# Issuing a two-layer attention and expert kernel's second attention in the written order

## The chip, the cores and the metric

The kernel runs on one core of one Trainium2 chip. The metric is the device time of one execution in microseconds, the median of the runs. Engines are named as the profile names them: PE (matmuls and transposes), DVE (VectorE), ACT (ScalarE), POOL (GpSimd), SP (SyncE, which here only issues DMAs). Each has its own queue of instructions and works through it in order; an instruction that has to wait for another engine or a DMA holds back whatever stands behind it in the same queue.

## The reference

Four blocks in a row are added to x, which has 4 batches of 512 rows of 256 numbers, in f32. ctx is a context of 4 batches of 1601 rows.

```python
x = x + L0_xattn(ctx, layernorm(x))   # 8 heads of 128, keys from context and x
x = x + L0_ffn(layernorm(x))          # top-2 of 8 experts, with a capacity for each
x = x + L1_xattn(ctx, layernorm(x))   # 8 heads of 32, keys from the context
x = x + L1_ffn(layernorm(x))          # top-2 of 8 experts by a threshold, no capacity
```

The change lies in the third, the second attention: q = layernorm(x) Wq, k = ctx Wk, v = ctx Wv, eight heads of 32, softmax over 1601 keys, no output projection.

## The kernel before, in words

Stage a is the first attention, stage b the first experts, stage c the second attention, stage d the second experts. PE ends stage b at 1927 us of the span. The change concerns stage c, and the work of its neighbours that runs inside it.

**Units and rounds.** The second attention is cut into 16 units: 4 batches, two groups of four heads (o), two halves of the queries (f, 256 each). A unit has NM = 13 key tiles of 128. A loop advances by two key tiles at a time; here one pass is called a round, and there are 104 of them with weights in them. Its counter, step, counts key tiles over all units.

**What a round holds.** `weights(u, j)` multiplies keys by queries into a PSUM tile ps_w (L1119) and ACT takes Exp of it into pT (L1132). The row maximum enters through an extra row of the queries (`asked`), so that ACT's Exp needs no further operand. `weigh` (L1150) multiplies pT, one round later, with v into ps_o. `add_weights` (L1141) adds pT to a running sum for the softmax's denominator, on DVE for the even tiles and on POOL for the odd tiles 3 to 11. pT has six buffers. `maxima(u, g)`, eight for each unit and done during the unit before, computes the scores of a quarter of the keys into two PSUM tiles ps_s (L1072), which DVE reduces to maxima (L1080). When a unit's eight are there, `negated` (L1089) reduces them to `shift`, and `to_row` (L1102, L1106) transposes them on PE and copies the row into `asked` on ACT. ps_s, ps_w and the PSUM tiles of the side work all come from one pool of three two-bank buffers (ps_s, tag s); the smaller ones of the closing come from a single buffer (ps_m).

**Closing.** When a unit's keys are done, `closing` copies ps_o (L1162), sums the denominators on PE (ps_n, L1168), copies them (by, L1177), transposes both (tp_o, L1182 and L1183), and on DVE takes reciprocals (L1192), scales (got, L1194) and adds to x (L1201).

**Side work, dealt out by step.** `put` and `spread` place generators' pieces in a table `at` by step: `collect` clears 8 tiles (L284) and gathers the first experts' results of the next batch into them with indirect DMAs on POOL (L285), `add_collected` adds them to x on DVE (L301), `queries` normalizes x (L93 to L116), transposes it (L130) and projects it (ps_q, L1021). `keys_values` of batches 2 and 3 (L873, L889) also runs here. `route2` is the second experts' routing of a batch whose attention is done: layernorm into `pay`, with a number of the lane beside it (L354, L362), transposes, scores (ps_l, L372), the choice of two experts in some thirty small DVE operations (L394 to L429), counts on PE (ps_c, L432), the places (L441 to L444), eight indirect DMAs on POOL that scatter `pay` to rows_x in DRAM (L446), and a bias through PE (L459 to L470).

**What sets the order.** SP's, PE's, DVE's, ACT's and POOL's instructions are traced in the order that the loop writes them, and a scheduler then orders each engine's queue by its own expectation of times. So the written order is a suggestion: what has no dependency may be moved up far ahead of its place. Sizes of instructions and buffers are as written.

Of the kernel before, what the change touches and what calls it, by code (L numbers as in the profile page):

```python
# [16 lines left out]
P = 128  # L17
# [44 lines left out]


@with_exitstack
def xattn_ffn_twice(ctx: ExitStack, tc: tile.TileContext, a: dict, out: bass.AP):
    nc = tc.nc

# [3 lines left out]
    ident = const.tile([P, P], F32, name="ident")  # L71
    make_identity(nc, ident)

# [26 lines left out]

    def ln_scale(pool, mv, n):
        ve = pool.tile([P, n], F32, tag=f"ve{n}", name="ve")
        nc.vector.tensor_scalar(ve, mv[:, :, 1], EPS, None, ALU.add)
        rs = pool.tile([P, n], F32, tag=f"rs{n}", name="rs")
        nc.scalar.activation(rs, ve, AF.Sqrt)
        nc.vector.reciprocal(rs, rs)

        t = pool.tile([P, n], F32, tag=f"nt{n}", name="t")
        nc.vector.tensor_tensor(t, rs, rs, ALU.mult)
        nc.vector.tensor_tensor(t, t, ve, ALU.mult)  # L110
        nc.vector.tensor_scalar(t, t, -0.5, 1.5, ALU.mult, ALU.add)
        nc.vector.tensor_tensor(rs, rs, t, ALU.mult)
        return mv, rs
# [163 lines left out]
    def collect(b):  # L277

        got = []
        for t in range(NT):  # L280
            for k in range(2):
                j = b * NT + t
                g = gat.tile([P, D], F32, tag="g", name="g")
                nc.vector.memset(g, 0.0)  # L284
                nc.gpsimd.indirect_dma_start(  # L285
                    out=g,
                    out_offset=None,
                    in_=slot_y[:, :],
                    in_offset=bass.IndirectOffsetOnAxis(ap=slot[k][:, j : j + 1], axis=0),
                    bounds_check=SLOTS - 1,  # L290
                    oob_is_err=False,
                )
                got.append(g)
        return got

    def add_collected(b, got):
        for t in range(NT):
# [49 lines left out]
    def route2(b, two, psum, tag, first=0, n=NT):  # L347
# [40 lines left out]

        yield

# [14 lines left out]

        yield

# [14 lines left out]

        yield

# [12 lines left out]
        )  # L437
        yield
        for k in range(2):
# [15 lines left out]
        yield  # L455

# [5 lines left out]
        for t0 in range(0, n, 2):  # L462
# [474 lines left out]
    with ExitStack() as st:  # L937
# [44 lines left out]

        got0 = collect(0)

# [6 lines left out]
    with ExitStack() as st:  # L991
# [19 lines left out]
        def queries(b, qT):  # L1011
            xn = one.tile([P, NT, D], F32, tag="xn", name="xn")
            layernorm(two, xn, x[b], NT)
            yield
# [143 lines left out]
        def closing(u, ps):  # L1158
# [3 lines left out]
            nc.scalar.copy(oT, ps)  # L1162
            yield
            ps = ps_m.tile([P, QH], F32, tag="m", name="ps_n")
            for k in range(2):
                for i in range(HG):
# [7 lines left out]
                    )  # L1174
            yield
            by = one.tile([P, QH], F32, tag="by", name="by")
# [4 lines left out]
            for t in range(2):  # L1181
# [7 lines left out]
                )  # L1189
            yield  # L1190
            inv = two.tile([P, 2 * HG], F32, tag="inv", name="inv")
# [102 lines left out]
        if to_close:  # L1294
            for _ in to_close:
                pass
        assert not at, sorted(at)

# [3 lines left out]
    with ExitStack() as st:  # L1302
# [151 lines left out]
        nc.vector.tensor_copy(n_over_i, n_over)  # L1454
        ties = nc.values_load(n_over_i[0:1, 0:1], min_val=0, max_val=E * T)
        spare = st.enter_context(tc.tile_pool(name="d_spare", bufs=1))
# [135 lines left out]
```

## Time and profile before

| | us |
|---|---|
| four runs | 3068.07, 3066.93, 3063.63, 3064.47 |
| median | 3065.7 |
| the profiled execution | 3066.01 |
| its span | 3064.3 |
| second attention, first weights to the last sums | 1996.0 to 2677.4 |

A profile is of one execution. Its page gives busy time of each engine, the chain of work and the costliest groups; the trace can be asked for windows, for the waits of an engine and for single instructions in order of time. A timeline row reads: start and duration in us, engine, line, operation, out<-in, sizes, count of instructions put together, and in brackets the idle time of that engine before it and what ended it. Line numbers are those of the kernel before.

### The profile page before, as it was taken

The numbers are of one execution on the slowest core, as the hardware profiler recorded it, in microseconds if no ns is written. First come the engines' busy times: TensorE is split into PE (matmuls) and PEld (weight loads), VectorE is DVE, ScalarE is ACT, GpSimd is POOL, SyncE is SP. The second block draws the span as 40 slices with busy tenths as digits, with TensorE's granted clock in tenths as the row PEclk, the third lists the DMA queues.
The fourth block names the chain that finished last, engine by engine and source line by source line (L and its number), as shares of the span: only waits on it lengthen the run. The fifth ranks groups of instructions, "written<-read, shape, count | busy, mean of one in ns | idle before, by whom it ended". The sixth has DMA issues, their size and how long they took to land. (4 is left out here: it accounts for less than half of the span.)

```text
span 3064.3 us, 35871 instructions
## 1 busy us (share of the span) xinstructions
PE 2833.9 (92%) x13564; PEld 1888.0 (62%) x13564; DVE 1436.5 (47%) x2351; ACT 932.7 (30%) x1328; POOL 476.0 (16%) x347
## 2 busy tenths in 40 slices
PE   5899999999999999999997999599989897859999
PEld 2566666666666667666664666344544444448888
DVE  4365456544565454454443000677657566621111
ACT  2233234233342333323221211144344343412221
POOL 1000000100001000010001000333333333434442
PEclk9999999999999999999997999699999898869999
DMA  8543343344433433333333331300010100045562
GB/s 301 182 115 99 99 109 89 103 101 101 110 89 102 103 95 92 87 106 99 92 99 117 120 110 57 84 16 18 17 44 15 34 15 23 12 159 186 171 194 72
DMA packets 160941, 293.94 MB, mean 96 GB/s; under 512 B 42824, under 2 KB 78014, under 8 KB 157560
## 3 DMA queue, kind: packets, MB, share of 16 engines
q1 hardware_dynamic: 118280, 181.12, 21.4%
q0 software_dynamic: 17904, 74.77, 7.7%
q10 hardware_dynamic: 24576, 35.68, 4.4%
q8 instruction: 108, 1.77, 0.2%
q14 instruction: 73, 0.60, 0.1%
HBM read 100.24 MB, written 42.69 MB: 47 GB/s over the span
## 5 line engine op out<-in xcount | busy, mean ns | idle before, releaser
L687 DVE TENSOR_REDUCE top<-ps_s 128x1 f32<-128x2113 f32 x128 | 301.8, 2358 | 580.9 <-PE ps_s L679 577.5
L716 PE MATMUL ps_o<-pT,v 128*128 128x256 f32 x2176 | 521.2, 382 | 7.9 <-DVE pT L708 7.9
L679 PE MATMUL ps_s<-kT,qT 128*128 128x512 f32 (+1 forms) x1280 | 489.6, 527 | 14.8 <-ACT attn L693 14.5
L716 PEld LDWEIGHTS ps_o<-pT,v 128*128 128x128 f32 x2176 | 411.1, 191 | 125.0 <-issue 69.9
L679 PEld LDWEIGHTS ps_s<-kT,qT 128*128 128x128 f32 x1280 | 242.0, 191 | 264.5 <-issue 240.1
L693 ACT ACTIVATE attn<-ps_s,top 128x2113 f32<-128x2113 f32 x128 | 259.0, 2024 | 475.4 <-DVE top L687 412.5
L708 DVE STREAM_TRANSPOSE pT<-swapped 128x2176 f32<-128x2176 f32 x128 | 312.4, 2441 | 58.2 <-DMA swapped<-attn 47.9
L1080 DVE TENSOR_REDUCE tops<-ps_s 128x2 f32<-128x800 f32 (+1 forms) x256 | 243.2, 983 | 87.3 <-PE ps_s L1072 86.9
L1119 PE MATMUL ps_w<-asked,keyed 64*128 64x256 f32 (+1 forms) x1664 | 244.8, 426 | 39.8 <-DVE tops L1080 38.3
L629 PE MATMUL ps_k<-kvin,wkv 128*128 128x512 f32 (+1 forms) x640 | 261.5, 533 | 4.3 <-ACT kT L636 4.3
L1141 POOL TENSOR_TENSOR sum<-sum,pT 128x1024 f32<-128x1024 f32 x80 | 200.2, 2503 | 395.0 <-PE ps_o L1150 206.0
L662 PE MATMUL ps_v<-wkv,kvin 128*128 128x256 f32 x1088 | 253.5, 381 | 0.0
L1132 ACT ACTIVATE pT<-ps_w 128x1024 f32<-128x1024 f32 (+1 forms) x176 | 176.6, 1023 | 223.9 <-PE ps_w L1119 222.0
L1119 PEld LDWEIGHTS ps_w<-asked,keyed 64*128 64x128 f32 (+1 forms) x1664 | 157.4, 197 | 133.8 <-DVE tops L1080 74.1
L662 PEld LDWEIGHTS ps_v<-wkv,kvin 128*128 128x128 f32 x1088 | 204.9, 190 | 32.7 <-issue 3.3
L1072 PE MATMUL ps_s<-kT,qT 32*128 32x400 f32 (+1 forms) x1024 | 162.1, 588 | 26.7 <-DVE tops L1080 24.5
L1141 DVE TENSOR_TENSOR sum<-sum,pT 128x1024 f32<-128x1024 f32 x96 | 141.1, 1469 | 92.7 <-ACT pT L1132 79.5
L636 ACT ACTIVATE kT<-ps_k,bqk 128x512 f32<-128x512 f32 (+1 forms) x160 | 97.2, 621 | 267.0 <-PE ps_k L629 121.2
L629 PEld LDWEIGHTS ps_k<-kvin,wkv 128*128 128x128 f32 x640 | 116.2, 191 | 80.1 <-issue 67.0
L1417 PE MATMUL ps_h<-xT,w_e 128*128 128x256 f32 x736 | 163.7, 381 | 0.0
L1436 PE MATMUL ps_y<-w_e,hT 128*128 128x256 f32 x736 | 162.5, 379 | 0.0
L1417 PEld LDWEIGHTS ps_h<-xT,w_e 128*128 128x128 f32 x736 | 140.7, 191 | 19.3
(239 smaller groups left out, 2611.1 us busy)
## 6 DMA issues: line engine op xcount, KB each, us to landing
swapped<-attn SPq DMA_DIRECT2D x1536, 68.0 KB
swapped<-attn ACTq DMA_DIRECT2D x512, 68.0 KB
rows_x<-empty SPq DMA_DIRECT2D x32, 530.0 KB
w<-in_w_dram SPq DMA_DIRECT2D x16, 1024.0 KB
cT<-in_ctxT_dram SPq DMA_DIRECT2D x4, 1601.0 KB
keyed<-kT SPq DMA_DIRECT2D x32, 200.1 KB
ctx_b<-in_ctx_dram SPq DMA_DIRECT2D x4, 1536.0 KB
slot_x<-empty POOLq DMA_DIRECT2D x8, 512.0 KB
```

Of the source, the lines that this page charges most:

```text
L629: nc.tensor.matmul(ps[:, :n], lhsT=wkv[:, c, hs], rhs=flat_kvin[c][:, j0 : j0 + n], start=c == 0, stop=c == DC - 1,)
L662: nc.tensor.matmul(ps[:, k, :], lhsT=flat_kvin[c][:, j * P : (j + 1) * P], rhs=wkv[:, c, cols], start=c == 0, stop=c == DC - 1,)
L679: nc.tensor.matmul(flat[:, j0 : j0 + n], lhsT=qT[:, t * P : (t + 1) * P], rhs=kT[:, j0 : j0 + n], start=True, stop=True,)
L687: nc.vector.tensor_reduce(top, flat[:, :L], AX.X, ALU.max, negate=True)
L693: nc.scalar.activation(attn[:, :L], flat[:, :L], AF.Exp, bias=top, accum_out=total)
L708: nc.vector.transpose(pT[:, :, k * P : (k + 1) * P].rearrange("p c (a i) -> p a c i", a=4), swapped.rearrange("p a (c i) -> p a c i", i=32),)
L716: nc.tensor.matmul(ps, lhsT=v[:, j - parts[part][0], (h % 2) * DH0 : (h % 2 + 1) * DH0], rhs=pT[:, j, :], start=j == 0, stop=j == NB - 1,)
L1080: nc.vector.tensor_reduce(tops[u][:, t, 2 * pair : 2 * pair + 2, k], pss[pair][:, :, : hi - lo], AX.X, ALU.max,)
L1119: nc.tensor.matmul(ps[:r, s, pair * QH : (pair + 1) * QH], lhsT=keyed[o][64 * s : 64 * s + 64, pair, j * P : j * P + r], rhs=asked[u % 3][ ...
L1132: nc.scalar.activation(pT[:r], ps[:r], AF.Exp)
L1141: (nc.gpsimd if k else nc.vector).tensor_tensor(to, to, pT[:r], ALU.add)
L1417: nc.tensor.matmul(ps[:, f, :], lhsT=w[:, at : at + P], rhs=xT[:, c, :], start=c == 0, stop=c == DC - 1,)
```

## The change

An object with the four engines takes the place of `nc` and, while a flag is set, tells the scheduler of every instruction traced on PE, DVE, ACT and POOL that it has to stay behind the one traced before it on its engine. The flag is set from the first unit's maxima to the end of the second attention's loop. SP's DMAs are not held. The write order in the loop is changed with it: of a round's maxima the first stands ahead of the weights and the others behind them, and the adds of pT stand one round earlier and ahead of `weigh`. Closing is done in three pieces, at its step, 4 and 6 steps later. `to_row` stands one step earlier. `collect` is dealt out one gather to a step, `add_collected` one tile to two steps, and `queries` and `route2` are cut at other places, mostly where work passes from one engine to another, and dealt out one piece to two steps: `queries` in 5 pieces from step 22 of a batch (4 from 18), `route2` in up to 16 from step 10 (8, one to a step, from 12), with one scatter to a piece. All from the softmax's weights (L400) over the choice of experts and the counts on PE to the places, which were in four pieces before, is now one piece.

```diff
+class InOrder:
...
+    def __getattr__(self, name):
+        f = getattr(self.engine, name)
+        def call(*args, **kwargs):
+            ins = f(*args, **kwargs)
+            if self.kept[0]:
+                self.tc.keep_in_program_order(ins)
+            return ins
+        return call
...
 def xattn_ffn_twice(ctx: ExitStack, tc: tile.TileContext, a: dict, out: bass.AP):
-    nc = tc.nc
+    nc = Engines(tc)
...
-    def ln_scale(pool, mv, n):
+    def ln_root(pool, mv, n):
         ve = pool.tile([P, n], F32, tag=f"ve{n}", name="ve")
         nc.vector.tensor_scalar(ve, mv[:, :, 1], EPS, None, ALU.add)
         rs = pool.tile([P, n], F32, tag=f"rs{n}", name="rs")
         nc.scalar.activation(rs, ve, AF.Sqrt)
+        return ve, rs
+
+    def ln_scale(pool, mv, n, root=None):
+        ve, rs = root or ln_root(pool, mv, n)
         nc.vector.reciprocal(rs, rs)
...
     def collect(b):
...
+        return got, [lambda t=t, k=k: one_of(t, k) for t in range(NT) for k in range(2)]
...
-        mv, rs = ln_stats(two, xb, n)
+        mv = ln_moments(two, xb, n)
+        root = ln_root(two, mv, n)
+        yield
+        mv, rs = ln_scale(two, mv, n, root)
...
-        yield
 
         lg, wb, keep, rest = wide("lg"), wide("wb"), wide("keep"), wide("rest")
...
         nc.scalar.activation(wb, wb, AF.Exp)
+        yield
         nc.vector.tensor_tensor(wb, wb, keep, ALU.mult)
...
         nc.vector.tensor_copy(pay[:, :, D + 1 :], wb)
 
-        yield
 
         nc.vector.tensor_copy(rest, keep)
...
         nc.vector.tensor_tensor(extra[:, mine_b, :], rest, wb, ALU.mult)
 
-        yield
...
             ps.rearrange(flat), lhsT=ones, rhs=earlier.rearrange(flat), start=False, stop=True
         )
-        yield
         for k in range(2):
             off, place, at = small("off2"), wide("place"), place2[k][:, mine_b]
...
             nc.vector.tensor_copy(at, off)
+        yield
+        for k in range(2):
+            at = place2[k][:, mine_b]
             for t in range(n):
                 nc.gpsimd.indirect_dma_start(
...
-
-        yield
+                yield
+
...
             nc.vector.tensor_tensor(xs, xs, ps, ALU.add)
+            yield
...
         for u in range(1, n_units):
-            for g in range(2 * HG):
-                put(NM * u - 5 - NM + (g * NM) // (2 * HG), lambda u=u, g=g: maxima(u, g))
             put(NM * u - 5, lambda u=u: negated(u))
-            put(NM * u - 3, lambda u=u: to_row(u))
+            put(NM * u - 4, lambda u=u: to_row(u))
...
-                spread(s0 + 12, route2(b - 1, one, ps_s, "s"))
+                spread(s0 + 10, route2(b - 1, one, ps_s, "s"), 2, 16)
             if b + 1 < B:
-                got = []
-                put(s0 + 1, lambda b=b, got=got: got.extend(collect(b + 1)), lambda b=b: begin(b + 1))
-                put(s0 + 16, lambda b=b, got=got: add_collected(b + 1, got))
+                put(s0 + 1, lambda b=b: begin(b + 1))
+                got, steps = collect(b + 1)
+                for k, f in enumerate(steps):
+                    put(s0 + 1 + k, f)
+                for t in range(NT):
+                    put(
+                        s0 + 14 + 2 * t,
+                        lambda b=b, got=got, t=t: add_collected(b + 1, got, (t,)),
+                    )
...
-                spread(s0 + 18, later(), 2, 4)
+                spread(s0 + 22, later(), 2, 5)
...
-        spread(per_batch * (B - 1) + 2 * NM + 12, last_half, 1, 8)
+        spread(per_batch * (B - 1) + 2 * NM + 11, last_half, 1, 14)
...
+        nc.kept[0] = True
         for g in range(2 * HG):
             maxima(0, g)
         negated(0)
         to_row(0)
-        for step in sorted(k for k in at if k < 0):
-            for f in at.pop(step):
-                f()
+
+        ahead = {}
+        for u in range(1, n_units):
+            for g in range(2 * HG):
+                step = NM * u - 5 - NM + (g * NM) // (2 * HG)
+                ahead.setdefault(max(step, 0) // 2, []).append((u, g))
 
         held = []
-        to_add = []
-        to_close = None
-        for step in range(0, NM * n_units + 6, 2):
+        for step in range(0, NM * n_units + 10, 2):
+            first, *more = ahead.pop(step // 2, [None])
+            if first:
+                maxima(*first)
             fresh = []
             for k in range(step, step + 2):
                 u, j = divmod(k, NM)
                 if u < n_units:
                     fresh.append((u, j, weights(u, j)))
-            if to_close:
-                if next(to_close, 1):
-                    to_close = None
+            for g in more:
+                maxima(*g)
+            for h in held:
+                add_weights(*h)
             for uw, jw, pT in held:
...
                 if jw == NM - 1:
-                    to_close = closing(uw, ps_of)
-                    next(to_close)
-            for h in to_add:
-                add_weights(*h)
+                    ending = closing(uw, ps_of)
+                    next(ending)
+                    put(step + 4, lambda ending=ending: next(ending))
+                    put(step + 6, lambda ending=ending: next(ending, None))
...
-            held = to_add = fresh
+            held = fresh
...
+        nc.kept[0] = False
```

The new names: `ahead` holds the maxima by round, and `ending` a closing's generator. Those maxima that fall ahead of the first step go to round 0. Apart from order, the instructions are the same ones.

More of the change, by code (lines that the diff above doesn't have):

```diff
@@ L61, in rows_of, with __init__ @@
     return tail if i == n - 1 else P
+class InOrder:
+    def __init__(self, tc, engine, kept):
+        self.tc, self.engine, self.kept = tc, engine, kept
+    def __getattr__(self, name):
[6 more added lines that the diff above has]
+        return call
+class Engines:
+    def __init__(self, tc):
+        self.kept = [False]
+        self.tensor, self.vector, self.scalar, self.gpsimd = (
+            InOrder(tc, e, self.kept) for e in (tc.nc.tensor, tc.nc.vector, tc.nc.scalar, tc.nc.gpsimd)
+        )
+        self.sync = tc.nc.sync
 @with_exitstack
 def xattn_ffn_twice(ctx: ExitStack, tc: tile.TileContext, a: dict, out: bass.AP):
-    nc = tc.nc
+    nc = Engines(tc)
     const = ctx.enter_context(tc.tile_pool(name="const", bufs=1))
@@ L71, in xattn_ffn_twice @@
     ident = const.tile([P, P], F32, name="ident")
-    make_identity(nc, ident)
+    make_identity(tc.nc, ident)
     flip = [0]
@@ L279, in collect, with one_of, add_collected @@
         got = []
[L280 to L297, printed above, removed]
+        def one_of(t, k):
+            j = b * NT + t
+            g = gat.tile([P, D], F32, tag="g", name="g")
+            nc.vector.memset(g, 0.0)
+            nc.gpsimd.indirect_dma_start(
+                out=g,
+                out_offset=None,
+                in_=slot_y[:, :],
+                in_offset=bass.IndirectOffsetOnAxis(ap=slot[k][:, j : j + 1], axis=0),
+                bounds_check=SLOTS - 1,
+                oob_is_err=False,
+            )
+            got.append(g)
+        return got, [lambda t=t, k=k: one_of(t, k) for t in range(NT) for k in range(2)]
+    def add_collected(b, got, tiles=range(NT)):
+        for t in tiles:
             for k in range(2):
@@ L981, in xattn_ffn_twice @@
         results(*last)
-        got0 = collect(0)
+        got0, steps = collect(0)
+        for f in steps:
+            f()
     QH = 2 * P
@@ L1012, in queries @@
             xn = one.tile([P, NT, D], F32, tag="xn", name="xn")
-            layernorm(two, xn, x[b], NT)
+            mv = ln_moments(two, x[b], NT)
+            root = ln_root(two, mv, NT)
+            yield
+            mv, rs = ln_scale(two, mv, NT, root)
+            for i in range(NT):
+                ln_apply(xn, x[b], mv, rs, i)
             yield
@@ L1174, in closing @@
                     )
-            yield
             by = one.tile([P, QH], F32, tag="by", name="by")
@@ L1189, in closing @@
                 )
-            yield
             inv = two.tile([P, 2 * HG], F32, tag="inv", name="inv")
@@ L1229, in xattn_ffn_twice @@
                 put(s0, lambda b=b: load_keys(b, 1))
-                spread(s0 + 12, route2(b - 1, one, ps_s, "s"))
+                spread(s0 + 10, route2(b - 1, one, ps_s, "s"), 2, 16)
             if b + 1 < B:
-                got = []
-                put(s0 + 1, lambda b=b, got=got: got.extend(collect(b + 1)), lambda b=b: begin(b + 1))
-                put(s0 + 16, lambda b=b, got=got: add_collected(b + 1, got))
+                put(s0 + 1, lambda b=b: begin(b + 1))
[6 more added lines that the diff above has]
+                        lambda b=b, got=got, t=t: add_collected(b + 1, got, (t,)),
+                    )
                 def later(b=b):
                     yield from queries(b + 1, qTs[b + 1])
-                spread(s0 + 18, later(), 2, 4)
+                spread(s0 + 22, later(), 2, 5)
             if 1 <= b and b + 1 < B:
@@ L1292, in xattn_ffn_twice @@
                     f()
-            held = to_add = fresh
[L1294 to L1297, printed above, removed]
+            held = fresh
+        assert not at and not ahead, (sorted(at), sorted(ahead))
+        nc.kept[0] = False
     kvst.close()
@@ L1454, in xattn_ffn_twice @@
         nc.vector.tensor_copy(n_over_i, n_over)
-        ties = nc.values_load(n_over_i[0:1, 0:1], min_val=0, max_val=E * T)
+        ties = tc.nc.values_load(n_over_i[0:1, 0:1], min_val=0, max_val=E * T)
         spare = st.enter_context(tc.tile_pool(name="d_spare", bufs=1))
```

## The prediction

> **What bounds the kernel now.** I read the busy line first, then the windows around the second attention, then single rounds in the timeline, then PE's and DVE's waits.
>
> ```profile
> span 3064.3 us, 35871 instructions
> PE 2833.9 (92%) x13564; PEld 1888.0 (62%) x13564; DVE 1436.5 (47%) x2351; ACT 932.7 (30%) x1328; POOL 476.0 (16%) x347
> ```
>
> PE sets the span. The profiled execution took 3066.01 us, 1.7 more than its span and 0.3 more than the median 3065.7, so a change of the span carries over to the median as it is. About 0.2%, 6.1 us, is what a measurement of this kernel can tell from no change. The next view has, after each window, PE, PEld, DVE, ACT, POOL busy, the granted clock, DMA share and GB/s.
>
> ```profile
> 1927.00:1963.00 36.00, 7.70 (x22) 3.71 (x24) 18.96 (x65) 8.77 (x8) 17.83 (x18) 0.57 0.44 117
> 1963.00:1996.00 33.00, 29.09 (x102) 11.16 (x98) 30.66 (x72) 3.11 (x5) 14.95 (x15) 0.57 0.22 61
> 1996.00:2670.00 674.00, 603.72 (x5006) 330.38 (x5004) 449.21 (x688) 272.92 (x330) 224.58 (x106) 0.93 0.08 22
> ```
>
> The experts end at 1927, the first weights' matmul is at 1996, the last units' end is near 2677. In the long window PE idles 674.0 − 603.7 = 70.3 us; to that I add the 6.4 us stop at 2677 shown below, 77 in all. At clock 0.93 its 603.7 us hold about 561 of full-speed work, so slow clock costs 43. Only these two sums, and the 69 us of start, can be won or enlarged; the matmuls stay the same ones.
>
> An undisturbed round (two key tiles):
>
> ```profile
> 2009.86 0.95 PE L1072 MATMUL ps_s<-kT,qT 32*128 32x400 f32 x8
> 2010.75 2.29 PE L1119 MATMUL ps_w<-asked,keyed 64*128 64x256 f32 x16
> 2012.96 1.07 PE L1150 MATMUL ps_o<-pT,v 128*32 128x256 f32 x16
> 2013.96 0.96 PE L1072 MATMUL ps_s<-kT,qT 32*128 32x401 f32 x8
> ...
> 2010.85 1.89 DVE L1080 TENSOR_REDUCE tops<-ps_s 128x2 f32<-128x800 f32 x2 [0.74 <-PE ps_s L1072]
> 2012.98 1.22 DVE L1141 TENSOR_TENSOR sum<-sum,pT 128x1024 f32<-128x1024 f32 x1 [0.24 <-ACT pT L1132]
> ```
>
> By starts, PE spends 0.89 + 2.21 + 1.00 = 4.10 us. DVE needs 1.89 + 1.22 = 3.11, so about 0.9 us more DVE work in a round is free; what exceeds it makes PE wait, because scores and weights share three PSUM buffers.
>
> **The stalls there are.** DVE's waits name the largest, "pay<-lane" behind a scatter, 20.2 us in 3 times; two of them with PE's answer:
>
> ```profile
> 2417.15 0.33 DVE L362 TENSOR_SCALAR pay<-lane 128x1 f32<-128x1 f32 x4 [8.59 <-DMA rows_x<-pay,place]
> 2418.44 1.72 PE L1072 MATMUL ps_s<-kT,qT 32*128 32x400 f32 x8 [7.70 <-DVE tops L1080]
> ...
> 2604.48 0.21 DVE L362 TENSOR_SCALAR pay<-lane 128x1 f32<-128x1 f32 x2 [8.40 <-DMA rows_x<-pay,place]
> 2605.65 0.69 PE L1119 MATMUL ps_w<-asked,keyed 64*65 64x256 f32 x2 [10.19 <-DVE tops L1080]
> ```
>
> The scheduler hoisted a few-element write of the next routing far ahead; it waits until the previous scatters have read the buffer, and the reduces queue behind it. PE loses 2.30 (at 2234) + 7.70 + 10.19 = 20.2. After the 7.70 the same scores last 1.72 for 0.95: the clock halved, some 3 us more each time. The end:
>
> ```profile
> 2677.36 1.08 PE L1168 MATMUL ps_n<-sum,ones 128*32 128x256 f32 x8 [6.40 <-POOL sum L1141]
> ```
>
> Three POOL adds (7.5 us) run late behind scatters.
>
> **Part 1, the start.** Pinning ends the hoisting of later batches' gathers, memsets and layernorms into 1948–1994. The first LN's own steps from sqrt (1948.6) to transposes (1955.4) take 6.8 us of which 2.1 are its own DVE work up to the first scaled tile, and the transposes follow a like step later: −5.4. The 16 first reduces ran 1964.97 to 1986.88, 21.9 us; back to back 16 × 0.95 = 15.2: −6.7. Before, 13 maxima preceded the first weights; written order has 9, which takes the rest. First weights at about 1977 instead of 1996, −18.7. But four maxima now follow, 4 × 0.89 = +3.6, and round 0 holds five of them, whose reduces (5 × 1.89) outlast PE's work by 4.3. Net **−10.8**.
>
> **Part 2, lane waits and the end.** The write now stands in its routing, long after the previous scatters: 20.2 of idle go, and two clock tails. POOL's last adds: written order leaves the scatters of the last half-routing two rounds to finish; 1 of 6.4 stays. Both are in the sum of part 3.
>
> **Part 3, new waits.** A DVE instruction that waits for something now holds its place, and what stands behind it, mostly the two reduces, waits too. By the same DVE balance (from single durations: reduce 0.95, add 1.22, PE 4.10):
> - Rounds with two maxima, one before and one after the weights: 15 of them have no key/value projection to cover them; the second maxima's scores start 0.89 + 2.21 = 3.10 into the round, their reduces 0.99 later as above, 4.09 to 5.98, and the add ends at 7.20; the next round's scores start at 4.10 + 0.89 = 4.99 and could be reduced from 5.98. DVE is 1.22 late, and PE, out of buffers, waits as long: 15 × 1.25 = 19. The trace has such stops of 0.42 (PE's scores at 2094.76) and 1.19 (weights at 2090.66).
> - 16 closings: reciprocal 0.20, got 0.42, x add 0.42 to 2.00 between the reduces; less the free 0.9: 0.35 to 2.0, taken 0.8: 13.
> - The shift's maximum and its row now stand one step apart, often in one round: PE's transposes wait for DVE's last reduces. 7 rounds × 1.5 + 6 × 0.5 = 13.5.
> - The routing's choose chain, in one piece with PE's ps_c in its middle: 27 small DVE operations stand before ps_c, at about 0.17 each (the small rows of the layernorm lasted 0.10 to 0.20) 4.6 us. Before, its last part took 2194.18 to 2199.2, one of its operations lasting 2.35. In written order PE arrives and waits: 3 × 4.6 + the half routing with 5.3, a lock's part in it, = 19.
> - The other pieces (layernorms of three batches 5 + 2 × 3.4, routing scores 2 × 1.4 + 2.6, wbT 3 × 0.8, halves 5): 25.
> - POOL's end: 1.
> Sum 91 of idle against the 77 before: **+14**, the 20 us of lane waits being in the 77. Before has no such rows in this order, so each is bounded by 0 (side work on PE's queue covers it) and by about double (a lock in it, as the 2.35 above); no gain is possible from a wait added.
>
> **Part 4, the clock.** Four choose stalls × 3.1 = +12, lane tails −6, and PE waits less deep in its ordinary rounds: −6 taken from the 43. Net 0. The gathers, dealt one per step, I cost at nothing: their readers stand 13 steps behind the first and 12 behind the last, 25 us, and DMA share is 0.08. On POOL two gathers of 1.01 and an add of 2.35 make 4.36 in a round of 4.10, so its adds slip by 1 us over four rounds, which six pT buffers cover; without that cover it is 1 us of PE in each of three batches. SP's loads are not pinned and stand five rounds ahead of their use. Scatters stay 2.8 to 2.9 us each on POOL; their price is the last rival's.
>
> Sum: −10.8 + 14 + 0 = **+3.3: 3066 + 3 = 3069 us**, own range 3050 to 3088.
>
> [...]
>
> **Rivals.** *Faster, 3030:* adds are issued one round earlier, and collide less with POOL. Undisturbed adds take 1.22, those of the stage have mean 1.44 (79 of them), 17 us of DVE time. Units without side work took 34.8 to 37.0 us from one ps_n to the next, where 6.5 rounds × 4.10 = 26.7, 1.5 more maxima at 0.89, and 2 to 3 us of the closing's own matmuls make 31. If 8 such units fall by 3 (−24) and half-clock windows (27 × 3.41 us) lose a third, −15: −39 from 3069. For it: PE's waits on the reduces, 38.3 + 23.6. Against it: POOL's adds stay as many and as long.
>
> *Slower, 3105:* the lock.
>
> ```profile
> 2087.07 2.35 POOL L1141 TENSOR_TENSOR sum<-sum,pT 128x1024 f32<-128x1024 f32 x1 [1.75 <-ACT pT L1132]
> ...
> 2087.71 2.00 DVE L1201 TENSOR_TENSOR x<-x,got 128x256 f32<-128x256 f32 x1
> ```
>
> The x add (0.42 alone, mean 1.15 over 16) ends when the POOL add ends. In the written order both adds of a round start as the two exps end, so that a closing's x add, 2 rounds later, meets POOL each time: 16 × 1.2, and the adds of 15 double rounds × 0.55, 27 us; with clock tails of five half-rate windows, 5 × 3.1 = 16, and less 7 of the 13 that I counted for closings, +36 on 3069. It decides if the x adds' mean passes 1.15. [...]
>
> *Not what it says, 3093:* in the built order, POOL's scatters are not held behind adds: four stand in a row, 4 × 2.9 = 11.6 us before the next add; the six pT buffers, three rounds of work or 12.3 us, are then nearly used up, and ACT and after it PE would wait some 3 us in each of four routings, a clock tail of 3.1 behind it: 4 × 6 = +24.
>
> **Chances.** Own forecast 0.50 (of it 0.14 faster by over 0.2%, 0.14 within, 0.22 slower), faster rival 0.27 (0.01 of it within), lock 0.18, scatters 0.05. Faster 0.40, same 0.15, slower 0.45. The range reaches from below the faster rival to just above the lock: 3022 to 3108.
>
> **What would show it.** First weights near 1977; "pay<-lane" gone from DVE's waits; ps_c waited for about 4.6 three times; PE's transposes of the shift waiting behind double rounds; idle of the stage near 91; its last ps_n near 2680. Wrong if idle stays under 60 (faster), if x adds average over 1.15 us or clock falls below 0.91 (lock), or if PE waits for pT while POOL scatters.

## The result, and the profile after

The changed kernel takes 3071.4 us (median of 45 runs, 3061.07 to 3077.18) where the kernel before takes 3067.5 (68 runs); the ratio is 1.0011, with a 95% interval of 1.0005 to 1.0016. By the ratio that is 3.4 us more (the medians differ by 3.9), inside the 0.2% that the prediction called no change. The profiled execution took 3071.08.

The page's head and busy line:

```profile
span 3069.4 us, 35856 instructions
PE 2822.9 (92%) x13564; PEld 1878.8 (61%) x13564; DVE 1455.3 (47%) x2351; ACT 941.3 (31%) x1332; POOL 466.1 (15%) x347
```

The span is 5.1 us longer, and PE is busy 11 us less: time has gone into waiting. The windows, split at the first weights and at the last sums (columns as before):

```profile
1927.00:1969.92 42.92, 24.14 (x93) 11.18 (x93) 25.53 (x50) 10.25 (x10) 8.24 (x8) 0.60 0.28 72
...
1969.92:2682.50 712.58, 608.99 (x5044) 326.02 (x5044) 493.92 (x776) 283.01 (x338) 246.21 (x132) 0.91 0.09 24
```

The first weights come at 1969.9 instead of 1996.0, 26.1 us earlier. From there to the last sums PE idles 712.58 − 608.99 = 103.6 us, where it was 77. So the changed kernel is 26 us ahead at the first weights, loses 27 in waits behind them, and carries four more maxima there. The start, PE's and DVE's rows:

```profile
1944.13 2.14 PE L74 MATMUL tp<-ident,xn 128*128 128x128 f32 x8 [21.07 <-DVE xn L74]
...
1969.92 3.35 PE L74 MATMUL ps_w<-asked,keyed 64*128 64x256 f32 x16
...
1982.26 3.79 PE L74 MATMUL ps_w<-asked,keyed 64*128 64x256 f32 x16
...
1952.20 14.89 DVE L74 TENSOR_REDUCE tops<-ps_s 128x2 f32<-128x800 f32 x16 [5.84 <-PE ps_s L74]
```

Nothing of later batches stands between; the 16 reduces run back to back in 14.9 us. Not all of the 26 us is the change's, though. The idle time ahead of the transposes begins where PE ends the experts, at 1944.13 − 21.07 = 1923.06 here, and in the kernel before at 1927.29:

```profile
1955.42 2.14 PE L130 MATMUL tp<-ident,xn 128*128 128x128 f32 x8 [28.13 <-DVE st L93]
```

Seven of the variants below have the changed kernel's code up to there, and in their profiles the experts end at 1924.7 to 1927.5, so I take these 4.2 us for the spread between executions. Counted from the experts' end, the first weights come after 46.9 us instead of 68.7, 21.8 less, and the last sums after 759.4 us instead of 750.1, 9.3 more (the kernel before, then the changed one):

```profile
1927.29:2677.40 750.11, 640.90 (x5132) 345.44 (x5134) 501.34 (x827) 285.18 (x343) 264.51 (x140) 0.89 0.10 28
...
1923.06:2682.50 759.44, 633.13 (x5132) 337.20 (x5136) 520.09 (x827) 293.59 (x347) 254.45 (x140) 0.90 0.10 28
```

The first round lasts from 1969.92 to 1982.26, 12.3 us. It has five maxima's scores in it and no `weigh` yet: 2.21 + 5 x 0.89 = 6.7 us of work. The profile has PE idle for 0.24 us of it only, but in its middle DVE sets the pace:

```profile
1974.40:1979.40 5.00, 5.00 (x24) 1.79 (x24) 5.00 (x6) 0.00 (x0) 0.00 (x0) 1.00 0.00 0
...
1974.19 7.28 DVE L74 TENSOR_REDUCE tops<-ps_s 128x2 f32<-128x800 f32 x8 [2.28 <-PE ps_s L74]
...
1976.13 0.30 PEld L74 LDWEIGHTS ps_s<-kT,qT 32*128 32x128 f32 x4 [0.60 <-DVE tops L74]
```

The scores of four maxima go on from 1974.40 to 1982.26, 7.9 us for 3.6, and up to 1979.4 at a full clock: the weight load (PEld) of each group of four waits for a reduce, and DVE works without a gap. These 4.3 us are a wait for DVE that is counted as busy time of PE. The weights ahead of them ran at a clock of 0.58, 3.28 us for 2.21. And PE's waits (total, times, longest):

```profile
PE ps_w L74 <- DVE tops L74: 41.6, 30, 4.9
PE ps_c L74 <- DVE earlier L74: 17.8, 6, 5.6
PE ps_r L74 <- DVE shift L74: 16.3, 9, 3.0
PE tp L74 <- DVE pay L74: 6.5, 2, 4.1
PE ps_o L74 <- ACT oT L74: 6.2, 8, 0.8
PE ps_c L74 <- DVE cnt L74: 4.4, 1, 4.4
```

The 7.7 to 10.2 us stops behind the lane's write are gone, and so is the wait of DVE for the scatters. In their place stand many stops of up to 5.6 us, of the kinds shown all but one behind DVE.

### The profile page after: what moved, and what is told of

It is laid out like the page before. It is cut to its first block, busy times and chain, and to the rows that moved or that the text cites. A ratio compares the mean times of both kernels' runs of the same rounds, so it can differ in the third digit from the quotient of the medians.

```text
span 3069.4 us, 35856 instructions
## 1 busy us (share of the span) xinstructions
PE 2822.9 (92%) x13564; PEld 1878.8 (61%) x13564; DVE 1455.3 (47%) x2351; ACT 941.3 (31%) x1332; POOL 466.1 (15%) x347
## 5 line engine op out<-in xcount | busy, mean ns | idle before, releaser
L74 PE MATMUL ps_s<-kT,qT 128*128 128x512 f32 (+3 forms) x2304 | 633.9, 554 | 18.2 <-ACT attn L74 14.7
L74 PE MATMUL ps_o<-pT,v 128*128 128x256 f32 (+2 forms) x3584 | 626.8, 395 | 7.7 <-DVE pT L74 7.7
L74 PEld LDWEIGHTS ps_o<-pT,v 128*128 128x128 f32 (+2 forms) x3584 | 450.2, 161 | 179.1 <-issue 111.0
L74 PEld LDWEIGHTS ps_s<-kT,qT 128*128 128x128 f32 (+1 forms) x2304 | 292.8, 193 | 320.8 <-issue 264.9
L74 PE MATMUL ps_w<-asked,keyed 64*128 64x256 f32 (+1 forms) x1664 | 252.5, 432 | 49.5 <-DVE tops L74 41.6
L74 ACT COPY v<-ps_v 128x512 f32<-128x512 f32 (+1 forms) x165 | 91.6, 560 | 278.0 <-PE ps_v L74 210.5
L74 DVE TENSOR_TENSOR sum<-sum,pT 128x1024 f32<-128x1024 f32 x96 | 154.2, 1606 | 6.3 <-ACT pT L74 6.3
```

The costliest lines, as they stand in the source:

```text
L74: ins = f(*args, **kwargs)
```

## The experiments

Two theories were tried. One: instructions in fixed places move PE's waits, and their sum follows what DVE has to do in a round with PE's work of 4.1 to 5.0 us against it. The other: single badly placed instructions (PE's ps_c, the shift's row) cost what PE waits at them. Differences between kernels of different sets of runs are taken from their ratios to the kernel before, in parts of 3066 us.

### The adds' place in a round

```diff
-            for g in more:
-                maxima(*g)
             for h in held:
                 add_weights(*h)
+            for g in more:
+                maxima(*g)
```

> The changed kernel with DVE's and POOL's adds of pT written ahead of a round's second maxima and not behind them, so that in a round with two maxima DVE does reduce, reduce, add and then the second pair. The prediction's sum for such a round has DVE late by 1.22 us because its add comes after reduces that can't start before 4.09: by it the add falls into DVE's idle time from 2.9 to 4.1 and 15 x 1.25 = 19 us go: 3052. Rival (the add isn't ready then, because its Exp ends later, or the wait is the shift's): within 6 of the changed kernel.

3037.7 us, ratio 0.9918 (0.9901 to 0.9935): about 28 us less than the changed kernel by the ratios, and clearly faster than the kernel before. One such round in the changed kernel's timeline, DVE's rows first:

```profile
2086.68 1.89 DVE L74 TENSOR_REDUCE tops<-ps_s 128x2 f32<-128x800 f32 x2 [1.21 <-PE ps_s L74]
2087.03 2.35 POOL L74 TENSOR_TENSOR sum<-sum,pT 128x1024 f32<-128x1024 f32 x1 [3.65 <-ACT pT L74]
2088.48 1.98 DVE L74 TENSOR_TENSOR sum<-sum,pT 128x1024 f32<-128x1024 f32 x1
2090.38 0.23 DVE L74 TENSOR_REDUCE shift<-tops 128x4 f32<-128x16 f32 x2
2090.59 0.66 PE L74 MATMUL ps_r<-ident,shift 128*128 128x128 f32 x4 [2.95 <-DVE shift L74]
```

and the same round with the adds first:

```profile
2081.68 1.21 DVE L74 TENSOR_TENSOR sum<-sum,pT 128x1024 f32<-128x1024 f32 x1
...
2082.97 1.89 DVE L74 TENSOR_REDUCE tops<-ps_s 128x2 f32<-128x800 f32 x2
2083.32 2.35 POOL L74 TENSOR_TENSOR sum<-sum,pT 128x1024 f32<-128x1024 f32 x1 [3.65 <-ACT pT L74]
2084.77 0.23 DVE L74 TENSOR_REDUCE shift<-tops 128x4 f32<-128x16 f32 x2
2084.99 0.66 PE L74 MATMUL ps_r<-ident,shift 128*128 128x128 f32 x4 [1.05 <-DVE shift L74]
```

In the first, DVE idles 1.21 and then does its add when POOL's add runs, 1.98 for 1.21; in the second the add fills the idle time and meets no POOL add. PE's wait falls by 1.90, from 2.95 to 1.05. Over the stage (its window from the first weights to the last sums):

```profile
1971.40:2641.30 669.90, 589.16 (x5048) 317.90 (x5044) 490.00 (x776) 283.16 (x339) 252.71 (x132) 0.94 0.09 26
```

PE idles 80.7 us where it was 103.6, 22.9 less for the 19 that the prediction's term had. PE's busy time falls by 19.8 with the same matmuls, as the clock rises from 0.91 to 0.94. In these two executions the clock's part is nearly as large as the wait's own, and the expectation had none. But the profiled execution, 3030.5, is the fastest of its runs, 3030.5 to 3041.1, and the stage is 42.7 us shorter in it where the ratios give 28. The mean clock of a whole run is 0.962 to 0.964 in all six of them, and 0.955 to 0.962 in the changed kernel's, with a median of 0.959; 0.004 of 3050 us is 12 us, an estimate of the clock's part of the 28.

### The shift's row one step later, on top of it

```diff
-            put(NM * u - 4, lambda u=u: to_row(u))
+            put(NM * u - 3, lambda u=u: to_row(u))
```

> The changed kernel with the adds ahead of the second maxima, and the shift's row put back to one step later, as in the kernel before. In the changed kernel half of the units have the shift's maximum and the row's transposes in one round, so PE meets the transposes while DVE still reduces; 11.6 us in 9 places are left of that wait. Theory (it is only the place): they go, 3038 - 11 = 3027. Rival (PE then runs on to the next wait for DVE, which is as far behind): 3034 to 3038.

3038.4 us, ratio 0.9910 (0.9896 to 0.9924): no change against 0.9918. PE's waits at the row have fallen from 11.6 us to 1.2, and these have grown or come:

```profile
PE ps_w L74 <- DVE tops L74: 29.0, 23, 2.9
...
PE ps_s L74 <- DVE tops L74: 2.7, 2, 2.0
```

ps_w was 25.6, and ps_s behind DVE's reduces was not in the list. By the first weights of the last key tile PE has idled 77.2 us, 78.5 without the edit. The rival holds: PE runs on to the next place at which it needs DVE.

### The second unit's maxima dealt two to a round

```diff
-                ahead.setdefault(max(step, 0) // 2, []).append((u, g))
+                ahead.setdefault((g if u == 1 else step) // 2, []).append((u, g))
```

> The changed kernel with the adds ahead of the second maxima, and the second unit's eight maxima dealt two to each of the first four rounds, where the changed kernel has five in round 0 and one in the next three. In the changed kernel round 0 lasts 12.3 us where PE's work is 4.10 + 4 x 0.89 = 7.7. The prediction's step says that five pairs of reduces outlast PE's work and that this costs 4.3; with two maxima to a round DVE's 3.78 + 1.22 fits PE's 4.99: 3038 - 5 = 3033. Rival (the time there is the halved clock of a PE that waits anyway): 3038.

3033.8 us, ratio 0.9891 (0.9874 to 0.9907); its interval and the 0.9901 to 0.9935 without the edit overlap, so the median's 4 us are not shown. From the first weights to those of the second unit the trace takes 44.1 us, 43.7 without the edit. Taken by rounds, the theory holds where it was aimed: the first round takes 6.3 us instead of 11.6. That is 5.3 less for three maxima fewer, as much as their reduces take (3 x 1.8) and twice what PE's work on them would (3 x 0.89). (The expectation's 7.7 us of work has 1.0 for a `weigh` in it that this round lacks.) The halved clock of the rival was not the reason, as the row for the scores of four maxima without the edit shows, with PE and DVE both busy throughout at a clock of 1.00:

```profile
1975.91:1983.03 7.12, 7.12 (x32) 2.39 (x32) 7.12 (x9) 0.00 (x0) 0.00 (x0) 1.00 0.00 0
```

But the gain is lost at once: the next three rounds, with a maximum more in each, take 21.5 us instead of 12.7. Two maxima to a round don't fit there either, because of rows like these:

```profile
1987.96 1.01 POOL L74 DMA_INDIRECT g<-slot_y,slot  x1 [0.30 <-issue]
1988.31 4.16 DVE L74 TENSOR_TENSOR sum<-sum,pT 128x1024 f32<-128x1024 f32 x1
...
1989.00 2.38 POOL L74 TENSOR_TENSOR sum<-sum,pT 128x1024 f32<-128x1024 f32 x1
...
1993.42 0.94 PE L74 MATMUL ps_s<-kT,qT 32*128 32x400 f32 x4 [1.98 <-DVE tops L74]
```

DVE's add of 1.2 us lasts 4.16 (and again at 1996.47), over POOL's gather and then the whole of POOL's add, and PE stops behind the reduces that follow.

### The closing's add to x on POOL

```diff
-            nc.vector.tensor_tensor(
+            nc.gpsimd.tensor_tensor(
                 xs, xs, got.rearrange("p (t h) d -> p t (h d)", t=2), ALU.add
             )
```

> The changed kernel with the adds ahead of the second maxima, and the closing's add of its result to x put on POOL. On DVE that add lasts 0.42 alone and has a mean of 1.07 over 16 closings, 17 us in all, since it collides with POOL's adds of pT. Theory (in rounds with a closing DVE's total work against PE's 4.1 to 5.0 is what PE waits for, and the collisions are part of it): PE's wait falls by the prediction's 0.8 in each of 16 closings, 13 us, 3038 - 13 = 3025. Rival (on POOL the add takes its turn among POOL's adds and shuts DVE's adds out for as long, or POOL's adds come late for the closing's sums): 3034 to 3045.

3024.8 us, ratio 0.9872 (0.9854 to 0.9890): 13 to 14 us less than with the adds first alone, the fastest version here, 41 us under the kernel before. The add's rows by tile (min, median, max in ns), first with it on POOL:

```profile
L74 POOL TENSOR_TENSOR x<-x,got x16: 722/730/1646, 2042.1 to 2635.9; 128x256 f32<-128x256 f32 x16
```

and with it on DVE, adds first:

```profile
L74 DVE TENSOR_TENSOR x<-x,got x16: 424/936/3154, 2041.9 to 2643.7; 128x256 f32<-128x256 f32 x16
```

PE's waits behind the reduces, 25.6 us in 24 times, become 13.1 in 11: the 13 of the expectation. But the shift's waits grow from 11.6 to 15.1 and ps_c's by 2, so the traces' spans differ by 7.6 only; the rest of the medians' difference lies in the spread of the runs to compare with, whose profiled one is the fastest.

### The routing's chain of small operations

One cut ahead of PE's ps_c, and then three cuts:

```diff
+        yield          # chain_cut and chain_pieces
         ps = psum.tile([P, n, E], F32, tag=tag, name="ps_c2")
...
         nc.vector.tensor_copy(pay[:, :, D + 1 :], wb)
+        yield          # chain_pieces
...
         nc.vector.tensor_tensor(extra[:, mine_b, :], rest, wb, ALU.mult)
+        yield          # chain_pieces
```

> The changed kernel with one more cut in the routing, just ahead of PE's ps_c, so that PE meets ps_c one round after DVE begins the chain of small operations. Theory A (what costs is that PE's queue holds an instruction whose input is 5 us away): the waits for ps_c, 20.3 us in four places, go and some 10 us of halved clock behind them, 3071 - 30 = 3041. Rival B (what costs is the 4.6 us of DVE work in one piece against 0.9 us free in a round, whichever instruction of PE meets it): the waits move to ps_w or ps_s behind DVE's reduces, of much the same length, and the time stays within 6 of the changed kernel's 3071.

3065.4 us, ratio 1.0007 (0.9997 to 1.0018), within the 6 us of rival B, and not told apart from the changed kernel's 1.0011. The wait has moved as B says. The changed kernel's rows:

```profile
2200.39 2.85 POOL L74 TENSOR_TENSOR sum<-sum,pT 128x1024 f32<-128x1024 f32 x1 [5.12 <-ACT pT L74]
2200.96 2.33 DVE L74 TENSOR_TENSOR wb<-wb,keep 128x32 f32<-128x32 f32 x1
...
2206.75 0.60 PE L74 MATMUL ps_c<-cnt,before 128*128 128x32 f32 x2 [5.55 <-DVE earlier L74]
```

and with the cut, one round on:

```profile
2210.95 2.19 DVE L74 TENSOR_TENSOR taken<-taken,cnt 128x8 f32<-128x8 f32 x1
...
2215.43 2.08 PE L74 MATMUL ps_w<-asked,keyed 64*128 64x256 f32 x8 [5.95 <-DVE tops L74]
```

5.55 at ps_c have become 5.95 at ps_w. The sums say the same: PE's waits at ps_c fall from 22.2 us to 2.9, and those behind the reduces rise from 41.6:

```profile
PE ps_w L74 <- DVE tops L74: 56.1, 35, 6.9
```

Of the chain, 2 us are the first operation, which lasts 2.33 for 0.19 beside POOL's add.

> The changed kernel with the routing's chain of small operations cut in four (behind the softmax's weights, behind the choice, ahead of ps_c), one piece to two steps, 1 to 2 us of DVE work in each. Theory B of the run before it (DVE's excess over the free part of a round) gives about 1 us of wait for each piece that exceeds 0.9, some 6 us in place of 22, and no stall long enough for the clock: 3071 - 16 - 8 = 3047. Theory A gives the same 3041 as for the single cut; A and B part at the single cut.

3069.1 us, ratio 1.0011 (1.0000 to 1.0023): no change, and both theories' numbers were wrong. One round with a piece in it:

```profile
2212.72 2.33 DVE L74 COPY rest<-keep 128x32 f32<-128x32 f32 x1
...
2217.22 1.00 DVE L74 SCALAR_TENSOR_TENSOR x<-g,prob,x 128x256 f32<-128x256 f32 x2
...
2218.83 2.41 DVE L74 TENSOR_TENSOR x<-x,got 128x256 f32<-128x256 f32 x1
...
2222.35 2.08 PE L74 MATMUL ps_w<-asked,keyed 64*128 64x256 f32 x8 [5.00 <-DVE tops L74]
```

The piece (the copy, 2.33 us for 0.17 beside a POOL add, and then 2215.09 to 2217.2) shares its round with two collected adds, 1.0, with a closing whose x add lasts 2.41 beside POOL, and with the shift. A smaller piece brings nothing in a round that is full already; I had counted each piece alone. (That stops below some length leave the clock alone was my assumption; no run shows it.) Over the whole stage the waits at ps_c are gone, and others have grown by about as much: the reduces by 6.2, the routing's bias by 7.3 and its layernorm by 3.0, and the last sums wait 4.0 for POOL:

```profile
PE ps_w L74 <- DVE tops L74: 47.8, 30, 5.8
...
PE ps_b L74 <- DVE wbT L74: 10.5, 4, 3.4
PE tp L74 <- DVE pay L74: 9.5, 2, 5.4
```

Why the bias waits longer was not followed up.

### What the fixed places cost, and what one of them brings

The new written order with the scheduler free:

```diff
-        nc.kept[0] = True
```

> The changed kernel with its flag never set: the new written order and the new dealing, with the scheduler free again. Theory A (the instructions' fixed places carry both the gains, 26 us earlier first weights and no lane waits, and the losses, PE waiting for ps_c, for the shift and behind double rounds): without them the early write of the lane comes back and the ps_c waits of 22 us go, so about 3066, within 15 of the kernel before, with first weights near 1996 again. Rival B (the new dealing is what costs, whoever sets the order): slower than the kernel before by the 18 us of idle that the change added after its first unit, 3075 or more.

3061.6 us, ratio 0.9987 (0.9977 to 0.9998). Theory A's size, and B is out: the dealing itself costs nothing. The start is not quite A's: the first weights come at 1987.7 and not near 1996, 62.4 us behind the experts' end, where the kernel before takes 68.7 and the changed one 46.9. The lane's wait is back in DVE's list, longer than it ever was in the kernel before:

```profile
DVE pay L74 <- DMA rows_x<-pay,place: 34.2, 3, 13.0
```

The old written order, held:

```diff
-    nc = tc.nc
+    nc = Engines(tc)
...
+        nc.kept[0] = True
         for g in range(2 * HG):
             maxima(0, g)
...
+        nc.kept[0] = False
```

> The kernel before with its own written order, all four engines held to it from the first maxima to the end of the loop. Theory A: the lane waits go (-20 idle, -6 clock) and the start gains as in the changed kernel, but the undivided steps (8 gathers with their memsets at one step, 0.27 us each; four tiles added at one step; layernorm with its square root on ACT in one piece; eight scatters in one piece) stand in DVE's queue: 3085 to 3110. Rival B (the dealing costs nothing or is a loss): at or under 3071.

3073.2 us, ratio 1.0029 (1.0019 to 1.0039): between the two, under theory A's 3085. The first weights come 53.6 us behind the experts' end. PE waits 20.6 us in four places for the routing's layernorm and 24.0 in seven for ps_c; the undivided steps do stall it, but less than I thought.

One instruction held, in the kernel before:

```diff
-            nc.vector.tensor_scalar(
+            ins = nc.vector.tensor_scalar(
                 pay[:, t, D : D + 1], lane, float((b * NT + first + t) * P), None, ALU.add
             )
+            tc.keep_in_program_order(ins)
```

> The kernel before with one instruction held behind the one traced before it: the write of the lane's number into pay. Order on PE, ACT and POOL stays the same, on DVE only these writes move. Theory: the lane waits, 20.2 us of idle PE in three places and some 6 us of halved clock behind two of them, were a cost of the kernel before that nothing else covers: 3066 - 26 = 3040. Rival (cover): POOL's scatters are late behind the adds anyhow and the next wait in the queue takes their place; then 3060 to 3066.

3047.3 us, ratio 0.9943 (0.9922 to 0.9964): 17.5 us by the ratio, and the profiled span is 21.9 shorter. PE's idle time from the end of the experts to the last sums falls from 109.3 to 93.2 us, 16 of the 20.2; the other 4 came back as other waits. PE's busy time there falls by 7.3, for the 6 of halved clock in the theory. The order on PE, ACT and POOL is the same in both traces; on DVE some other instructions change places with the writes, so not every microsecond is theirs alone. This one held write does better than the whole change.

The same line in the changed kernel's order with the scheduler free:

> The changed kernel's written order and dealing with the scheduler free, and only the write of the lane's number held behind the instruction traced before it. With the scheduler free the three lane waits cost PE 12.36 + 9.15 + 8.90 = 30.4 us and a clock tail of some 3 each: 3061 - 30 - 8 = 3023. Rival (the waits hide other ones behind them, as the held order's 77 to 104 us of idle suggests): 3040 or more.

3035.4 us, ratio 0.9908 (0.9891 to 0.9924), 24 us under the free order without it. From 1927 to the last sums PE's idle time falls from 743.2 − 634.9 = 108.3 to 725.0 − 638.9 = 86.1, 22 us of the 30; a quarter came back as other waits, which the expectation had left out. PE's busy time rose by 4.0 in these two traces, and the profiled execution, 3040.9, is the slowest of its six.

All side work held and the loop free (the flag is set around each dealt-out piece alone, in the old order):

> The kernel before with only its side work held (gathers, collected adds, queries of later batches, routing, key and value projections: each instruction stays behind the one traced before it), and the main loop free to be scheduled. Theory A: no lane waits (-26) and nothing of later batches hoisted in front of the first maxima (-11), and the main loop may still pass a side instruction that waits: 3030. Rival B (held side work blocks DVE whatever is free around it): above 3060.

3070.4 us, ratio 1.0017 (1.0006 to 1.0027): rival B, by 40 us against theory A. PE waits 13 us at ps_c, and behind the reduces as long (41.5) as the kernel before does without its lane stops. The first weights come 53.8 us behind the experts' end, so the gain at the start is there, and the waits use it up. The loop's instructions were free to go ahead of a held one that waits, but the order that the scheduler made by its own expectation of times left these waits.

The adds first, held for the first batch only and then free, with the lane's write held:

```diff
+            if step == per_batch:
+                nc.kept[0] = False
             first, *more = ahead.pop(step // 2, [None])
```

> The changed kernel with the adds ahead of the second maxima, held to the written order only up to the end of the first batch; from there the scheduler is free, with the write of the lane's number alone held. Over the first four units the held order with adds first gained 16 us on the free one with the lane held, and over the last eleven the free one gained back 7. If these two parts add up: 3038 - 7 = 3031 or the free one's 3035 - 12 = 3023, so 3023 to 3031. Rival (the free scheduler hoists other work again once it is free, in the first batch too): 3035 or more.

3052.6 us, ratio 0.9959 (0.9946 to 0.9972): the rival. What is free is hoisted in front of what was held:

```profile
2054.38 4.70 DVE L74 SCALAR_TENSOR_TENSOR x<-g,prob,x 128x256 f32<-128x256 f32 x5
...
2059.11 3.12 DVE L74 SCALAR_TENSOR_TENSOR x<-g,prob,x 128x256 f32<-128x256 f32 x1
...
2064.41 1.22 PE L74 MATMUL ps_w<-asked,keyed 64*128 64x256 f32 x3 [8.39 <-DVE tops L74]
```

These are collected adds of the last two batches. All sixteen of them are done by 2063, in the second unit, where the changed kernel has them at 2187 to 2217 and 2375 to 2407; their gathers and they push DVE back, and PE stops for 8.39 us. Holding an instruction says nothing of what may come in front of it.

## Why the prediction was right, point by point

The total was right to a tenth of a per cent: +3.3 forecast, +3.4 measured. Part of that is luck. In this pair of executions the start brought 3 us more than forecast, and the waits cost 12.6 more. By what was measured the two add up to −13.9 + 26.6 = +12.7 us; counted from the experts' end the stage grew by 9.3, and where the other 3.4, busy time of PE, went is open. The 4.2 us ahead of the stage bring the difference of the spans down to 5.1, and the ratio of all runs gives 3.4. One pair of executions settles these terms to a few us only.

- **Start.** From the experts' end the first weights came 21.8 us earlier, 18.7 forecast. The reduces were right (15.2 forecast, 14.9 measured). The term for the first layernorm, −5.4, was a little small: its transposes came 21.07 us behind the experts' end instead of 28.13, 7.1 earlier. The sum began at the square root, and the hoisted work had delayed what lies ahead of it too. The step for the first round was right: its reduces outlast PE's work by 4.3, as forecast. Net −21.8 + 3.6 + 4.3 = −13.9 for −10.8.
- **Lane waits.** Gone, as forecast; holding that write alone in the kernel before shows their price, 17 by the ratio and 22 in the traces of 26. The end kept one stop of 2.1 us for the 1 forecast.
- **Waits of fixed places.** 91 us forecast, 103.6 measured. Behind the reduces: double rounds 19 and closings 13 forecast, 32 in all, 41.6 measured. The runs part the two: with the adds moved 16.0 of it goes, and with the x add on POOL another 12.5. ps_c: 19 and 22.2. The shift: 13.5 and 16.3. The other pieces and the end: 26 forecast, 17.3 left over. On top comes a wait that had no term at all, 6.2 us in eight places, where weigh of the next unit waits for the closing's copy out of the single ps_o buffer.
- **Clock.** Forecast no change. From the experts' end to the last sums PE is busy for 633.1 us where it was 640.9, with the same matmuls, at a mean clock of 0.90 for 0.89: 8 us less, with the 4.3 us in it by which DVE held up the first round. The stage's own clock fell from 0.93 to 0.91, and the shorter start made up for it. Behind the four stops at ps_c the clock reads 0.50 for 4.9, 7.7, 7.3 and 7.0 us from PE's restart, half of it lost, an estimate of 13 us for the 12 forecast; behind the two lane stops of the kernel before it reads so for 6.4 and 3.5 us, 5 lost for the 6. No run shows a tail of 3.1 us as a fixed price. For short stops the sum had no tail, and half a clock stood behind some of them too, as the last section shows.
- **Rivals.** Faster: the adds of pT on DVE did not come off POOL's adds, their mean over all 96 rose from 1.47 to 1.61 us. The stretches at half a clock, 27 of 3.41 us in the trace before from 2069.82 to 2639.85, became 33 (2027.32 to 2675.84). The adds' place mattered, as that rival says, but the other way: one round earlier they are not clear of POOL (31 of the 96 begin during a POOL add, 26 before), and having them behind the second maxima costs about 28 us. Slower: the x adds' mean is 1.11, under its mark of 1.15. What that rival calls the lock is in the changed kernel's trace an x add that ends 0.28 or 0.29 us behind POOL's add, in each of eleven that begin during one; it costs, but cost as much before (mean 1.15). Scatters in a row: PE waited for ACT's pT 2.6 us in all.
- **The choice chain.** Forecast 4.6 us, with no operation held up; measured 5.55, with 2.33 us for 0.19 in its first operation, beside POOL's add, so the number is in part luck: 20 of the 27 operations stand ahead of ps_c's first matmuls, 3.6 us without those 2, and the others cost PE a second wait of 0.6. In the fixed order POOL's add meets that operation in each of the three whole routings, 2.33 to 2.35 us; the half routing's lasts 0.18.

What the prediction did not see is that its own double-round term, 19 us of "DVE late by 1.22", was a slip in the written order that two lines mend, and that the clock adds to its price, about 28 us in all by the ratios.

## What to carry to other kernels

Add up each engine's work per round before work is dealt into rounds: what DVE had over PE's 4.1 to 5.0 us in a round was waited for in these runs, wherever the cuts stood and whichever of PE's instructions met it (5.55 us at ps_c became 5.95 at ps_w). Look for idle time of the bounding engine's partner within the round and write ready work there, as the adds ahead of the second maxima. Where one hoisted instruction makes a wait, hold that instruction: one held write brought 17 us where holding four engines in a new order brought a loss of 3. And read the waits of PE's weight loads beside PE's busy time: in the first round PE counted as busy for 4.3 us while DVE set its pace.

## What the runs showed of the hardware

In the changed kernel's trace 31 of the 96 adds of pT on DVE begin while a POOL add runs. Each of them ends 1.08 or 1.09 us behind that add, after 1.55 to 3.21 us, where an add alone takes 1.22; the one at 2088.48 lasts 1.98. The 128x32 product of 0.19 us at 2200.96 lasts 2.33, until 0.05 after the end of POOL's add. The copy of 128x32 at 2212.72 in the run with three cuts, with one input, lasts 2.33 as well, until 0.04 after it. The add of 4.16 us at 1988.31 in the run with two maxima to a round begins during a gather on POOL; POOL's add begins 0.69 us after it and ends 1.09 before it. What makes these operations last so long no run shows. On POOL the x add itself lasted 0.73 us (median) for 0.42 on DVE at its shortest, and the kernel was 13 us faster with it there.

Half a clock stood behind short stops as well. In the changed kernel the same eight matmuls of the weights last 1.14 us, and 1.91 right behind a stop of 2.39, where the clock reads 0.50 from 2044.38 to 2047.79:

```profile
2040.64 1.14 PE L74 MATMUL ps_w<-asked,keyed 64*128 64x256 f32 x8
2044.17 1.91 PE L74 MATMUL ps_w<-asked,keyed 64*128 64x256 f32 x8 [2.39 <-DVE tops L74]
```

Not so behind every stop: after one of 2.19 us (at 2004.18) the clock reads 1.00, and the next sixteen last their usual 2.29. With PE's idle time down by 22.9 us in the run with the adds first, and no stop over 5.6 in either kernel, its busy time for the same matmuls fell by 19.8 in the two executions compared. The prediction added clock tails only behind the routing's stops of some 4.6 us.
